# Attention maxima, depthwise taps and a scaling step: four edits in a fused block-and-attention kernel

## The chip, the cores and the metric

The kernel runs on one core of one Trainium2 chip. The time is the device time of one execution in microseconds (us). Engines are named as in the profile: TensorE is PE (its weight loads PEld), VectorE is DVE, ScalarE is ACT, GpSimd is POOL, and SyncE (SP) issues the transfers.

## What is computed

All data are float32. The input is `x` of shape (4, 64, 64, 256). Layer 0 is a block with a scan over windows of 2 x 2 pixels, a 3 x 3 depthwise convolution and a feed-forward part; layer 1 is full self-attention over the 4096 pixels of each image. Cut to what matters here (384 is the inner width):

```python
# layer 0
xz = layernorm(x) @ in_proj_W                 # 256 -> 2 x 384
x_proj, z = xz[..., :384], xz[..., 384:]
y_ssm  = 0.5 * (scan_fwd + scan_bwd)          # each: states over 4 pixels of a window, 8 states, plus x_proj * D
y_dw   = depthwise_3x3(x_proj)                # 9 taps per channel
y_conv = gelu(y_dw @ pw_W)
alpha  = sigmoid(gate)
y      = (alpha * y_ssm + (1 - alpha) * y_conv) * silu(z)
x_out  = x + y @ out_W
x1     = x_out + gelu(layernorm(x_out) @ fuse_W1 + b1) @ fuse_W2 + b2
# layer 1, per image, n = 4096
f, g, h = x1 @ Wf + bf, x1 @ Wg + bg, x1 @ Wh + bh      # 32, 32 and 256 wide
attn = softmax(g @ f.T, axis=-1)
out  = gamma * ((attn @ h) @ Wo + bo) + x1
```

## The kernel before

**Chunks.** Layer 0 works on 32 chunks of 8 rows (512 pixels, `TOK`), eight per image. In most of it channels lie on partitions, in `KI` = 3 blocks of 128. A chunk goes through `head` (layer norm, input projection to `xc`), `prepare` (the scan's parameters), `scan` (24 steps for each direction), `merge` (the scan's result `y` is transposed back and added into `xc`), and, one chunk behind, `conv` and `tail`. `halo` copies `xc` into the padded tile `xp`, which the depthwise taps read.

**Depthwise.** `depthwise` treats the three channel blocks in turn. A block with `f < dense` is computed on TensorE: each tap is a matmul with a diagonal weight, accumulated in one PSUM bank, which ScalarE copies out (L571). The other blocks run on VectorE, nine operations per block (L580, L582), each adding one tap. In the first image two blocks are dense, afterwards one. Blocks and taps are told apart by the tiles of the profile's rows: `q<-xp,dw` is the first dense block, `q<-xp,wide` the second.

**Tail.** Pointwise matmul (L613), GELU (L618), a scaling by `1 - alpha` on ScalarE (L625), then on VectorE a combined multiply and add with `alpha / 2` times the scan's result (L628), the gate (L631), the output projection (L638, added at L642), the feed-forward part (L658, L669, L673) and the projections that attention reads (`fgd`, `vod` in DRAM, L682 to L699).

**Attention in tiles beside the layer.** As soon as the first image is through layer 0, attention starts and layer 0 of the next images runs beside it. A tile is 128 queries. `weights` makes a tile's 4096 x 128 scores (L832) in two groups of four banks, copies them to SBUF (L840), folds the maxima over keys (L846, L848, last fold L851), transposes them (L854), reduces (L856), broadcasts (L858), spreads them over partitions by a matmul with the identity (L860), copies that out as `nb` (L862), and then adds it and takes the exponential in four pieces (L866, L867). `attend` multiplies the finished weights with the values (L1027, 32 matmuls a tile) in eight steps.

**Order.** The order of issue is written out by Python generators: each `yield` gives the cost, in us, of what was just issued. In each of its eight steps `attend` issues four value matmuls, takes one piece of the next tile's `weights` (`next(beside, None)`), and lets `fill(RATE)` issue layer-0 work worth 7.2 by those costs. `weights` has eight pieces, so it is done when `attend` is. A scheduler then settles each engine's order from this issue order. PSUM banks `q0` to `q3` are handed out in turn by `aside()`; `four()` takes all four.

**Late pairs.** When layer 0 has ended (checked at even tiles), the remaining queries go in pairs of tiles, 256 queries at a time: `late_weights` (scores L924, copies L932, maxima L937 and L944, transposes L947, broadcast L954, spread L958, copy L961, bias and exponential L964, L965) and `attend_late` (L1005).

Every value block is loaded from DRAM for every tile (`vt<-vod`), by SyncE, four blocks ahead.

Of the kernel before, what the change touches and what calls it, by code (L numbers as in the profile page):

```python
# [22 lines left out]
AF = mybir.ActivationFunctionType  # L23
ALU = mybir.AluOpType
# [4 lines left out]
P = 128  # L29
# [5 lines left out]
KI = INNER // P  # L35
# [3 lines left out]
ROWS = 8  # L39
# [20 lines left out]
def block_then_attention_kernel(  # L60
# [97 lines left out]
    def aside(shape=(P, TOK)):  # L158

        i = turn[0]  # L160
        turn[0] = (i + 1) % 4
        return pss.tile(list(shape), F32, tag=f"q{i}", name=f"q{i}")
# [384 lines left out]
    def merge(at):  # L547

        y = merged.pop(at)
        xc = heads[at][1]  # L550
        for f in range(KI):
            py = bank()
            for t in range(4):
                nc.tensor.transpose(py[:, t * P : (t + 1) * P], y[:, t, f * P : (f + 1) * P], ident)
            nc.vector.scalar_tensor_tensor(xc[:, f, :], xc[:, f, :], dsum[:, f : f + 1], py, ALU.mult, ALU.add)
            yield 1.1

    def depthwise(ydw, dense):

        for f in range(KI):  # L560
            if f < dense:
                pc = aside()
                for tap in range(9):
                    dy, dx = divmod(tap, 3)
                    nc.tensor.matmul(  # L565
                        pc, lhsT=diags[9 * f + tap], rhs=xp[:, f, dy : dy + ROWS, dx : dx + W],
                        start=(tap == 0), stop=(tap == 8),
                    )
                    if tap in (2, 5):
                        yield 2.6  # L570
                nc.scalar.copy(ydw[:, f, :], pc)  # L571
                yield 2.6
                continue
            o = ydw[:, f, :].rearrange("p (r c) -> p r c", r=ROWS)
            for tap in range(9):
                dy, dx = divmod(tap, 3)
                x_tap = xp[:, f, dy : dy + ROWS, dx : dx + W]
                w_tap = v("dw", 9 * f + tap)
                if tap == 0:
                    nc.vector.tensor_scalar(o, x_tap, w_tap, None, ALU.mult)  # L580
                else:
                    nc.vector.scalar_tensor_tensor(o, x_tap, w_tap, o, ALU.mult, ALU.add)  # L582
                if tap % 3 == 2:
                    yield 2.0
# [3 lines left out]
    def conv(at):  # L588
        b = at // NBLK
        ydw = one.tile([P, KI, TOK], F32, tag="ff", name="ydw")  # L590
        ydws[at] = ydw
        yield from depthwise(ydw, KI - 1 if b == 0 else 1)

    def next_head(at):

# [6 lines left out]
    def tail(at):  # L602
# [7 lines left out]
        for f in range(KI):  # L610
# [10 lines left out]
                    AF.Gelu,  # L621
                )
            yield 2.58
        for f in range(KI):
            nc.scalar.activation(yz[:, f, :], yz[:, f, :], AF.Copy, scale=one_a[:, f : f + 1])  # L625

        for f in range(KI):
            nc.vector.scalar_tensor_tensor(  # L628
                yz[:, f, :], s[:, f, :], half_a[:, f : f + 1], yz[:, f, :], ALU.mult, ALU.add
            )  # L630
            nc.vector.tensor_tensor(yz[:, f, :], yz[:, f, :], zs[:, f, :], ALU.mult)  # L631
            yield 1.3
# [177 lines left out]
    def load_values(b, q, n):  # L810

        vt = vp.tile([P, 2, DIM + 1], F32, tag="vt", name="vt")
        a = 2 * (n % 2) * (DIM + 1)
        nc.sync.dma_start(
            out=vt.rearrange("p t c -> p (t c)"), in_=vod[b * NBLK + n // 2][:, a : a + 2 * (DIM + 1)]
        )
        vts[b, q, n] = vt

    def weights(b, q, es):


        fQ, gq = quarters[b], gqs.pop((b, q))
        mx = one.tile([P, TOK], F32, tag="mx", name="mx")
        for g in range(2):
            pr = four()

            with tc.high_priority():
                last = None
                for s in range(4):
                    at = g * TOK + s * P  # L830
                    for r in range(4):
                        ins = nc.tensor.matmul(  # L832
                            pr[r][:, s * P : (s + 1) * P], lhsT=fQ[CK * r : CK * (r + 1), at : at + P],
                            rhs=gq[CK * r : CK * (r + 1), :], start=True, stop=True,
                        )
                        last = behind(ins, last)
            for a in range(2):
                e = ep.tile([P, 2, TOK], F32, tag="eq", name="eq")
                for j in range(2):
                    nc.scalar.copy(e[:, j, :], pr[2 * a + j])  # L840
                es.append(e)
            yield
            for r in range(4):
                e = es[2 * g + r // 2]
                if g == 0 and r == 0:
                    nc.vector.tensor_tensor(mx, e[:, 0, :], e[:, 1, :], ALU.max)  # L846
                elif g == 1 or r > 1:
                    nc.vector.tensor_tensor(mx, mx, e[:, r % 2, :], ALU.max)  # L848
            if g == 0:
                yield  # L850
        nc.vector.tensor_tensor(mx[:, :QB], mx[:, :QB], mx[:, QB:], ALU.max)  # L851
        pm = aside()
        for c in range(2):
            nc.tensor.transpose(pm[:, c * P : (c + 1) * P], mx[:, c * P : (c + 1) * P], ident)  # L854
        nm = st.tile([P, 1], F32, tag="nm", name="nm")
        nc.vector.tensor_reduce(nm, pm[:, :QB], AX.X, ALU.max, negate=True)  # L856
        nmb = two.tile([P, P], F32, tag="nb", name="nmb")
        nc.vector.tensor_copy(nmb, nm.to_broadcast([P, P]))  # L858
        pn = aside()
        nc.tensor.matmul(pn[:, :P], lhsT=nmb, rhs=ident, start=True, stop=True)  # L860
        nb = two.tile([P, P], F32, tag="nb", name="nb")
        nc.scalar.copy(nb, pn[:, :P])  # L862
        yield
        for n, e in enumerate(es):
            e8 = e.rearrange("p r (s q) -> p (r s) q", s=4)
            nc.vector.tensor_tensor(e8, e8, nb.unsqueeze(1).broadcast_to([P, 8, P]), ALU.add)  # L866
            nc.scalar.activation(e, e, AF.Exp)  # L867
            yield
# [32 lines left out]
    def load_late_values(b, q, n):  # L901

        g, r = divmod(n, 4)
        vt = vp.tile([P, 2, DIM + 1], F32, tag="vt", name="vt")
        a = 2 * (g % 2) * (DIM + 1)
        nc.sync.dma_start(
            out=vt.rearrange("p t c -> p (t c)"),
            in_=vod[b * NBLK + 4 * (g // 2) + r][:, a : a + 2 * (DIM + 1)],
        )
        vts[b, q, n] = vt  # L910

    def late_weights(b, q, odd, es):
# [42 lines left out]
        yield  # L955
        pn = aside()
        for c in range(2):
            nc.tensor.matmul(  # L958
                pn[:, c * P : (c + 1) * P], lhsT=wide[:, c, :], rhs=ident, start=True, stop=True
            )  # L960
        nc.scalar.copy(nb, pn[:, :QB])  # L961
        for n, e in enumerate(es):
            e4 = e.rearrange("p r s q -> p (r s) q")
# [46 lines left out]
                next(beside, None)  # L1010
        outcome(b, 2 * q, res, sums)

    def attend(b, q, es, beside, following):

        res = load_rest(b, q, two, "res", 1)
        acc = pso.tile([P, TOK], F32, tag="pso", name="acc")
        for k in range(NI):
            for h in range(2):
                n = 2 * k + h
                if n + 4 < 2 * NI:  # L1020
                    load_values(b, q, n + 4)
                else:
                    following(n + 4 - 2 * NI)
                vt = vts.pop((b, q, n))
                for s in range(2):
                    a = (2 * h + s) * P
                    nc.tensor.matmul(  # L1027
                        acc[:, : DIM + 1], lhsT=es[k // 2][:, k % 2, a : a + P], rhs=vt[:, s, :],
                        start=(n == 0 and s == 0), stop=(n == 2 * NI - 1 and s == 1),
                    )  # L1030
            next(beside, None)
            fill(RATE)
        outcome(b, q, res, [acc])
# [17 lines left out]
    for n in range(4):  # L1051
        load_values(0, 0, n)
    es = []
    for _ in weights(0, 0, es):
        fill(RATE)
    a = 0
    while True:
        b, q = divmod(a, NQ)
        b1, q1 = divmod(a + 1, NQ)
        if q1 == 0:  # L1060
            until((b1 + 1) * NBLK - 1)
        ahead = []
        late = ready["tail"] == LAST - 1 and q1 % 2 == 0
        if late:
            n0 = (b1, q1 // 2)
            load_late_queries(*n0)
            beside = twice(late_weights(*n0, 0, ahead))
            attend(b, q, es, beside, lambda n: load_late_values(*n0, n))
            es = ahead
            break  # L1070
        if q1 == 0:
            quarter(b1, one, "fQ")
        load_queries(b1, q1)
        attend(b, q, es, weights(b1, q1, ahead), lambda n: load_values(b1, q1, n))
        es = ahead
        a += 1
    odd, block = 0, n0
    while block:
# [98 lines left out]
```

## Time and profile before

| | |
|---|---|
| three runs | 5365.54 us median (5365.16 to 5367.03) |
| the profiled execution's own time | 5371.37 us |
| its span, first to last instruction | 5369.6 us |
| busy: PE, DVE, ACT | 5029.3, 4558.3, 3599.4 us |
| mean granted TensorE clock | 0.978 |
| chunk 0 to the start of attention | about 0 to 940 us |
| attention beside layer 0 | about 940 to 4430 us |
| last two tiles without layer work | about 4430 to 4492 us |
| late pairs | about 4492 to 5369.6 us |

A row of the profile's groups reads: line, engine, operation, output<-inputs, shapes, count, then busy us and mean ns of one, then the idle time of the engine just before such an instruction and what ended it. A float32 matmul shows as two instructions, a transpose as one. TensorE's busy time is modelled at the ends of matmuls, so a group's busy time (overlaps counted once) is the better measure of what it takes than its mean duration. A line of the waits reads: engine, tile and line that waited, `<-` what ended the wait, then us in total, times, longest.

### The profile page before, as it was taken

What the parts mean: (1) busy time and instruction counts of PE and PEld (TensorE: products, weight loads), DVE (VectorE), ACT (ScalarE), POOL (GpSimd) and SP (SyncE); (2) the same over time, 40 slices, a digit from 0 to 9 for tenths busy, and PEclk for the clock granted to TensorE, in tenths of its full rate; (3) what the DMA queues carried; (4) which work ended last, traced back from release to release, by engine and by line L of the source; (5) the groups of instructions that cost most, each with busy time, mean ns of one, the idle gap of its engine ahead of it and who ended that gap; (6) DMA issues with size and microseconds to landing.
All of it is one profiled execution on the core that took longest, in us unless ns stands there. A gap on an engine that the chain in (4) does not pass through costs nothing. (4 is left out here: it accounts for less than half of the span.)

```text
span 5369.6 us, 77772 instructions
## 1 busy us (share of the span) xinstructions
PE 5029.3 (94%) x27476; PEld 3585.9 (67%) x27476; DVE 4558.3 (85%) x8386; ACT 3599.4 (67%) x5530; POOL 206.0 (4%) x304
## 2 busy tenths in 40 slices
PE   7999999999999999999999999999999999999999
PEld 4555555666666666666666666666666667888887
DVE  7999999889988899889889998888998875666665
ACT  5767767778777677767777766767777744555554
POOL 0000000000000000000000000000000000000000
PEclk8999999999999999999999999999999999999999
DMA  1001001333333333333333333333343335555554
GB/s 47 26 30 31 19 25 31 98 109 107 115 113 112 114 112 114 118 115 107 111 116 111 115 116 107 114 114 113 102 123 113 110 116 165 146 146 146 146 146 138
DMA packets 333126, 558.45 MB, mean 104 GB/s; under 512 B 51904, under 2 KB 86976, under 8 KB 332736
## 3 DMA queue, kind: packets, MB, share of 16 engines
q1 hardware_dynamic: 330160, 551.52, 35.1%
q8 instruction: 217, 3.56, 0.3%
q10 hardware_dynamic: 2576, 1.97, 0.1%
q14 instruction: 173, 1.42, 0.1%
HBM read 494.49 MB, written 58.79 MB: 103 GB/s over the span
## 5 line engine op out<-in xcount | busy, mean ns | idle before, releaser
L1027 PE MATMUL acc<-vt,eq 128*128 128x257 f32 x4864 | 1234.2, 389 | 16.9 <-DVE res L975 13.0
L392 ACT ACTIVATE e<-dt,a_sc 128x384 f32<-128x384 f32 x1536 | 852.7, 611 | 347.0 <-PE bank L449 318.9
L1027 PEld LDWEIGHTS acc<-vt,eq 128*128 128x128 f32 x4864 | 891.1, 193 | 249.2 <-issue 116.6
L467 DVE SCALAR_TENSOR_TENSOR y<-p,bc,y 128x384 f32<-128x384 f32 x1536 | 948.8, 618 | 0.7
L449 PEld LDWEIGHTS bank<-ident,e 128*128 128x128 f32 x4320 | 524.3, 143 | 302.1 <-issue 125.7
L449 PE MATMUL bank<-ident,e 128*128 128x128 f32 x4320 | 647.8, 280 | 72.2 <-DVE p L461 29.3
L1005 PE MATMUL bank<-vt,eT 128*128 128x257 f32 x2496 | 625.8, 382 | 0.0
L476 DVE SCALAR_TENSOR_TENSOR h<-u,bc,p 128x384 f32<-128x384 f32 x1024 | 618.2, 621 | 0.1
L461 DVE TENSOR_TENSOR p<-bank,h 128x384 f32<-128x384 f32 x960 | 517.0, 552 | 52.4 <-PE bank L449 50.4
L1005 PEld LDWEIGHTS bank<-vt,eT 128*128 128x128 f32 x2496 | 467.1, 190 | 81.0 <-issue 12.9
L840 ACT COPY eq<-q 128x512 f32<-128x512 f32 x608 | 310.8, 593 | 179.7 <-PE q L832 166.4
L866 DVE TENSOR_TENSOR eq<-eq,nb 128x1024 f32<-128x1024 f32 x304 | 367.7, 1231 | 19.2 <-ACT nb L862 18.9
L867 ACT ACTIVATE eq<-eq 128x1024 f32<-128x1024 f32 x304 | 317.5, 1054 | 92.7 <-DVE eq L866 88.7
L937 DVE TENSOR_TENSOR mx<-mx,eT 128x512 f32<-128x512 f32 x364 | 252.0, 692 | 143.0 <-ACT eT L932 113.2
L848 DVE TENSOR_TENSOR mx<-mx,eq 128x512 f32<-128x512 f32 x456 | 317.0, 695 | 50.5 <-ACT eq L840 38.5
L932 ACT COPY eT<-q 128x512 f32<-128x512 f32 x416 | 213.2, 597 | 188.5 <-PE q L924 188.5
L392 ACT ACT_TABLE_LOAD x254 | 325.9, 1283 | 11.0 <-PE bank L449 6.8
L457 DVE SCALAR_TENSOR_TENSOR p<-bank,bc,u 128x384 f32<-128x384 f32 x480 | 294.1, 613 | 45.8 <-PE bank L449 45.6
L582 DVE SCALAR_TENSOR_TENSOR ydw<-xp,vec,ydw 128x512 f32<-128x512 f32 x448 | 325.4, 750 | 2.2
L613 PE MATMUL q<-ydw,wpw 128*128 128x512 f32 x576 | 269.3, 599 | 18.8 <-ACT eq L840 18.8
L964 DVE TENSOR_TENSOR eT<-eT,m 128x1024 f32<-128x1024 f32 x208 | 238.5, 1221 | 46.6 <-ACT m L961 46.6
L565 PE MATMUL q<-xp,dw 128*128 128x512 f32 x576 | 274.0, 597 | 2.4 <-ACT eq L840 2.4
(151 smaller groups left out, 7394.7 us busy)
## 6 DMA issues: line engine op xcount, KB each, us to landing
vt<-vod SPq DMA_DIRECT2D x1632, 257.0 KB, 2.8
vod<-vst SPq DMA_DIRECT2D x32, 514.0 KB, 4.4
xo<-in_x_dram SPq DMA_DIRECT2D x256, 64.0 KB, 2.7
xt<-in_x_dram SPq DMA_DIRECT2D x256, 64.0 KB, 1.9
x1d<-xo SPq DMA_DIRECT2D x32, 512.0 KB, 2.9
res<-x1d SPq DMA_DIRECT2D x76, 128.0 KB, 2.6
out_dram<-res SPq DMA_DIRECT2D x304, 32.0 KB, 1.6
fgd<-fg SPq DMA_DIRECT2D x32, 256.0 KB, 2.0
```

The costliest lines, as they stand in the source:

```text
L392: nc.scalar.activation(e[:, f, :], dts[d][:, f, lo : lo + 3 * P], AF.Exp, scale=a_sc[:, d, f * NST + n : f * NST + n + 1],)
L449: nc.tensor.transpose(pa[:, f * P : (f + 1) * P], es[d, n][:, f, off : off + P], ident)
L461: nc.vector.tensor_tensor(p, pa[:, :INNER], hs[d], ALU.mult)
L467: nc.vector.scalar_tensor_tensor(y[:, t, :], p, bc[:, t, d, NST + n : NST + n + 1], y[:, t, :], ALU.mult, ALU.add)
L476: nc.vector.scalar_tensor_tensor(hs[d], u[d][:, t, :], bc[:, t, d, n : n + 1], p, ALU.mult, ALU.add)
L582: nc.vector.scalar_tensor_tensor(o, x_tap, w_tap, o, ALU.mult, ALU.add)
L840: nc.scalar.copy(e[:, j, :], pr[2 * a + j])
L848: nc.vector.tensor_tensor(mx, mx, e[:, r % 2, :], ALU.max)
L866: nc.vector.tensor_tensor(e8, e8, nb.unsqueeze(1).broadcast_to([P, 8, P]), ALU.add)
L867: nc.scalar.activation(e, e, AF.Exp)
L1005: nc.tensor.matmul(sums[c][:, : DIM + 1], lhsT=e[:, r % 2, s, c * P : (c + 1) * P], rhs=vt[:, s, :], start=(n == 0 and s == 0), stop=(n == ...
L1027: nc.tensor.matmul(acc[:, : DIM + 1], lhsT=es[k // 2][:, k % 2, a : a + P], rhs=vt[:, s, :], start=(n == 0 and s == 0), stop=(n == 2 * NI ...
```

## The change

There are four edits.

1. `weights` gets a `yield` between the last fold of the maxima and their transposes. It then has nine pieces for eight steps. `attend` therefore receives the tile's own generator as `own` and takes its last piece in its first step, ahead of the next tile's first piece. The first tile's generator is still run to its end before the first `attend`, with one more `fill`.
2. The spread of the maxima over partitions is a TensorE transpose instead of a matmul with the identity as the moving operand, in `weights` and in `late_weights`.
3. In the second to fourth images the dense block does taps 0 to 6 on TensorE; taps 7 and 8 are done on VectorE, the first of them reading the bank. The copy L571 is left out there. The costs yielded change from three times 2.6 to 2.6, 2.6 and 2.0 per block. In the first image all nine taps stay on TensorE, with the copy issued after the third yield instead of before it.
4. `merge` ends with ScalarE scaling `xc` by `alpha / 2`; the scaling by `1 - alpha` in `tail` is left out, and VectorE's combined operation multiplies the GELU's result by `1 - alpha` and adds the scaled `xc`.

```diff
--- before.py
+++ after.py
@@ -554,30 +554,36 @@
                 nc.tensor.transpose(py[:, t * P : (t + 1) * P], y[:, t, f * P : (f + 1) * P], ident)
             nc.vector.scalar_tensor_tensor(xc[:, f, :], xc[:, f, :], dsum[:, f : f + 1], py, ALU.mult, ALU.add)
             yield 1.1
-
-    def depthwise(ydw, dense):
+        for f in range(KI):
+            nc.scalar.activation(xc[:, f, :], xc[:, f, :], AF.Copy, scale=half_a[:, f : f + 1])
+
+    def depthwise(ydw, dense, taps):
 
         for f in range(KI):
             if f < dense:
                 pc = aside()
-                for tap in range(9):
+                for tap in range(taps):
                     dy, dx = divmod(tap, 3)
                     nc.tensor.matmul(
                         pc, lhsT=diags[9 * f + tap], rhs=xp[:, f, dy : dy + ROWS, dx : dx + W],
-                        start=(tap == 0), stop=(tap == 8),
+                        start=(tap == 0), stop=(tap == taps - 1),
                     )
-                    if tap in (2, 5):
+                    if tap % 3 == 2:
                         yield 2.6
-                nc.scalar.copy(ydw[:, f, :], pc)
-                yield 2.6
-                continue
+                if taps == 9:
+                    nc.scalar.copy(ydw[:, f, :], pc)
+                    continue
             o = ydw[:, f, :].rearrange("p (r c) -> p r c", r=ROWS)
-            for tap in range(9):
+            for tap in range(taps if f < dense else 0, 9):
                 dy, dx = divmod(tap, 3)
                 x_tap = xp[:, f, dy : dy + ROWS, dx : dx + W]
                 w_tap = v("dw", 9 * f + tap)
                 if tap == 0:
                     nc.vector.tensor_scalar(o, x_tap, w_tap, None, ALU.mult)
+                elif f < dense and tap == taps:
+                    nc.vector.scalar_tensor_tensor(
+                        o, x_tap, w_tap, pc.rearrange("p (r c) -> p r c", r=ROWS), ALU.mult, ALU.add
+                    )
                 else:
                     nc.vector.scalar_tensor_tensor(o, x_tap, w_tap, o, ALU.mult, ALU.add)
                 if tap % 3 == 2:
@@ -589,7 +595,7 @@
         b = at // NBLK
         ydw = one.tile([P, KI, TOK], F32, tag="ff", name="ydw")
         ydws[at] = ydw
-        yield from depthwise(ydw, KI - 1 if b == 0 else 1)
+        yield from depthwise(ydw, KI - 1 if b == 0 else 1, 9 if b == 0 else 7)
 
     def next_head(at):
 
@@ -621,12 +627,10 @@
                     AF.Gelu,
                 )
             yield 2.58
-        for f in range(KI):
-            nc.scalar.activation(yz[:, f, :], yz[:, f, :], AF.Copy, scale=one_a[:, f : f + 1])
 
         for f in range(KI):
             nc.vector.scalar_tensor_tensor(
-                yz[:, f, :], s[:, f, :], half_a[:, f : f + 1], yz[:, f, :], ALU.mult, ALU.add
+                yz[:, f, :], yz[:, f, :], one_a[:, f : f + 1], s[:, f, :], ALU.mult, ALU.add
             )
             nc.vector.tensor_tensor(yz[:, f, :], yz[:, f, :], zs[:, f, :], ALU.mult)
             yield 1.3
@@ -849,6 +853,7 @@
             if g == 0:
                 yield
         nc.vector.tensor_tensor(mx[:, :QB], mx[:, :QB], mx[:, QB:], ALU.max)
+        yield
         pm = aside()
         for c in range(2):
             nc.tensor.transpose(pm[:, c * P : (c + 1) * P], mx[:, c * P : (c + 1) * P], ident)
@@ -857,7 +862,7 @@
         nmb = two.tile([P, P], F32, tag="nb", name="nmb")
         nc.vector.tensor_copy(nmb, nm.to_broadcast([P, P]))
         pn = aside()
-        nc.tensor.matmul(pn[:, :P], lhsT=nmb, rhs=ident, start=True, stop=True)
+        nc.tensor.transpose(pn[:, :P], nmb, ident)
         nb = two.tile([P, P], F32, tag="nb", name="nb")
         nc.scalar.copy(nb, pn[:, :P])
         yield
@@ -955,9 +960,7 @@
         yield
         pn = aside()
         for c in range(2):
-            nc.tensor.matmul(
-                pn[:, c * P : (c + 1) * P], lhsT=wide[:, c, :], rhs=ident, start=True, stop=True
-            )
+            nc.tensor.transpose(pn[:, c * P : (c + 1) * P], wide[:, c, :], ident)
         nc.scalar.copy(nb, pn[:, :QB])
         for n, e in enumerate(es):
             e4 = e.rearrange("p r s q -> p (r s) q")
@@ -1010,7 +1013,7 @@
                 next(beside, None)
         outcome(b, 2 * q, res, sums)
 
-    def attend(b, q, es, beside, following):
+    def attend(b, q, es, own, beside, following):
 
         res = load_rest(b, q, two, "res", 1)
         acc = pso.tile([P, TOK], F32, tag="pso", name="acc")
@@ -1028,6 +1031,7 @@
                         acc[:, : DIM + 1], lhsT=es[k // 2][:, k % 2, a : a + P], rhs=vt[:, s, :],
                         start=(n == 0 and s == 0), stop=(n == 2 * NI - 1 and s == 1),
                     )
+            next(own, None)
             next(beside, None)
             fill(RATE)
         outcome(b, q, res, [acc])
@@ -1051,7 +1055,8 @@
     for n in range(4):
         load_values(0, 0, n)
     es = []
-    for _ in weights(0, 0, es):
+    own = weights(0, 0, es)
+    for _ in own:
         fill(RATE)
     a = 0
     while True:
@@ -1065,14 +1070,15 @@
             n0 = (b1, q1 // 2)
             load_late_queries(*n0)
             beside = twice(late_weights(*n0, 0, ahead))
-            attend(b, q, es, beside, lambda n: load_late_values(*n0, n))
+            attend(b, q, es, own, beside, lambda n: load_late_values(*n0, n))
             es = ahead
             break
         if q1 == 0:
             quarter(b1, one, "fQ")
         load_queries(b1, q1)
-        attend(b, q, es, weights(b1, q1, ahead), lambda n: load_values(b1, q1, n))
-        es = ahead
+        beside = weights(b1, q1, ahead)
+        attend(b, q, es, own, beside, lambda n: load_values(b1, q1, n))
+        es, own = ahead, beside
         a += 1
     odd, block = 0, n0
     while block:
```

## The prediction

> **What bounds the kernel now.** I read the busy line of the page first, then the busy time by stage, then the waits inside the long middle stage, then the rows of the operations that the change touches.
>
> ```profile
> PE 5029.3 (94%) x27476; PEld 3585.9 (67%) x27476; DVE 4558.3 (85%) x8386; ACT 3599.4 (67%) x5530; POOL 206.0 (4%) x304
> ```
>
> TensorE (PE) is the busiest, VectorE (DVE) next. The stages differ, so the second view cuts the span at 940 us (attention starts beside the first layer), at 4430 us (the layer has ended) and at 4492 us (the late pairs start). The columns are length, then PE, weight loads, DVE, ACT and POOL busy, then granted clock and DMA share.
>
> ```profile
> 0.00:940.00 940.00, 845.98 (x3588) 525.06 (x3589) 868.24 (x1766) 666.51 (x1075) 55.78 (x87) 0.94 0.10 30
> 940.00:4430.00 3490.00, 3254.34 (x18459) 2304.22 (x18457) 3103.46 (x5784) 2476.72 (x3783) 150.22 (x217) 0.98 0.38 112
> 4430.00:4492.00 62.00, 58.36 (x353) 43.50 (x352) 33.74 (x50) 25.64 (x41) 0.00 (x0) 0.92 0.67 201
> 4492.00:5369.60 877.60, 870.65 (x5080) 713.11 (x5078) 552.87 (x788) 430.52 (x633) 0.00 (x0) 1.00 0.50 144
> ```
>
> The first stage is VectorE's (92% busy, PE 90%). The last is TensorE's alone (99%, DVE 63%). In the middle stage TensorE is at 93% and VectorE at 89%: TensorE leads, but relief of TensorE that is paid for on VectorE cannot count in full. TensorE's 236 us of idle time there, and ScalarE's (ACT) waits for TensorE, are read from the waits of that window (who waited for whom: us, times, longest).
>
> ```profile
> PE q L854 <- DVE mx L851: 37.3, 30, 3.2
> PE q L613 <- ACT eq L840: 18.8, 15, 2.3
> PE bank L449 <- DVE p L457: 16.7, 11, 2.4
> PE bank L449 <- DVE p L461: 15.6, 12, 2.9
> ...
> ACT nb L862 <- PE q L860: 88.5, 44, 5.7
> ...
> ACT ydw L571 <- PE q L565: 43.6, 20, 7.6
> ```
>
> TensorE's largest single wait is for the fold of the maxima (L851), in front of the transposes (L854). Two other lines matter: ScalarE stands 88.5 us before the copy that ends the spread of the maxima, and 43.6 us before the copy that ends a TensorE depthwise chunk. VectorE mostly runs behind TensorE: the output projection's add (L642) follows 12 matmuls of 128x256, yet waits for them only 9 times in 48.
>
> The rows of the operations concerned (count, then busy us and mean ns of one):
>
> ```profile
> L582 DVE SCALAR_TENSOR_TENSOR ydw<-xp,vec,ydw 128x512 f32<-128x512 f32 x448 | 325.4, 750 | 2.2
> L565 PE MATMUL q<-xp,dw 128*128 128x512 f32 x576 | 274.0, 597 | 2.4 <-ACT eq L840 2.4
> L625 ACT ACTIVATE yz<-yz,one_a 128x512 f32<-128x512 f32 x96 | 65.2, 716 | 0.4
> L860 PE MATMUL q<-ident,nmb 128*128 128x128 f32 x152 | 33.1, 300 | 6.0 <-DVE nmb L858 5.5
> L854 PE MATMUL q<-ident,mx 128*128 128x128 f32 x152 | 31.1, 287 | 37.7 <-DVE mx L851 37.5
> L571 ACT COPY ydw<-q 128x512 f32<-128x512 f32 x40 | 23.4, 584 | 63.8 <-PE q L565 63.8
> ```
>
> **What the Trainium skill says.** "Perfetto Trace Analysis", section "Transposes", asks that logical transposes use transpose and not a standard matmul, since a transpose skips arithmetic. The trace agrees: 76 spreads by matmul (L860) are 152 instructions and 33.1 us, or 0.436 us each; 152 transposes of the same shape (L854) are 152 instructions and 31.1 us, or 0.205 us each. "VectorE: DVE Perf Modes", section "The perf-mode tier table", puts fp32 two-tensor operations at 1x wherever the operand lies. The trace agrees that PSUM costs nothing extra: the merge's operation reads a bank and takes 747 ns (L555), the tap from SBUF takes 750. "TensorE: Matmul & The Clock Gate", section "Architectural detail: the array is 16× 32×32, not 1× 128×128", says that VectorE and ScalarE keep strict queue order; the two waits of ScalarE above show what that costs whatever stands behind.
>
> **The change part by part.** All sums are changes of the profiled run, 5371.4 us (span 5369.6). The median of the runs is 5365.5, 0.11% lower; I apply the changes to the median.
>
> *Two taps.* In chunks 8 to 31 (24 of 32), 2 of 9 dense taps leave TensorE. A tap is two instructions of the L565 row: 274.0 us over 288 taps is 0.951 us. 24 x 2 x 0.951 = **-45.7 us** of TensorE, all in the middle stage. VectorE gets 48 operations at 0.750: +36.0 us, 1.0% of that stage. ScalarE loses 24 copies at 0.584: -14.0 us, and the 43.6 us wait with them. VectorE's slack is 387 us there, but its queue is in order, so part of the 36 reaches TensorE as later data: bounds 0 and 36, I take half, **+18**. The first new operation reads the bank directly behind the last dense matmul. VectorE then waits where ScalarE did: bounds 0 and 24 x 43.6/20 = 52 us. I take 0, for VectorE runs behind and only one matmul, not three, is issued between the last step's end and the read. Behind it in VectorE's queue stand the scan's operations, for which TensorE's transposes (L449) and ScalarE's exponentials wait; the bank it holds is next wanted by the scores (L832).
>
> *Spread by transposes.* 76 spreads fall from 0.436 to 0.205: about 74 x 0.231 = -17.1. In the late pairs (L958) 52 spread matmuls of 15.9 us (0.306 each) become the kind of L947 (10.0 us for 52, 0.192): 54 x 0.114 = -6.1, on the engine that sets that stage. **-23.2 us**. Nothing is added.
>
> *The step.* The fold is issued one step earlier than transposes, reduction, broadcast, spread and copy. A tile takes 8 steps (47.3 us, so 5.9 a step), and VectorE has that long to finish the fold: the 37.3 us can go. What is late next is the spread, which waits for reduction and broadcast (0.42 + 0.22 us) on the same lagging queue; before, TensorE had already waited that lag out at L854. Bounds: 0 and -37.3 us; I take half, **-19**. The ninth step carries one bias add (1.23 us) and one exponential (1.05 us) into the next tile's first step. They are first read at its seventh, some 35 us later: 0, bounded by +2.3 us a tile if that cover failed. The step issues no DMA, passes none on SP and nothing on POOL; the value loads keep their places.
>
> *Scaling moved.* 96 activations of 0.716 us leave the tail and 96 enter the merge, so ScalarE's sum stands. VectorE's 9.8 us wait for L625 may go, with 13.8 us of unattributed waits at the same line. In the merge ScalarE waits for VectorE, with copies of the next chunk's inputs (L409) behind it: at most one 0.75 us operation a chunk, +24 us. Bounds -24 and +24; I take 0. The built program also has 6 fewer table loads of 1.28 us on ScalarE: 0.
>
> *Fewer tiles beside the layer.* The new steps count less cost (7.2 instead of 7.8 per dense chunk), and the first tile's ninth step draws layer work forward. In the built program the accumulations fall from 2432 to 2368, two tiles fewer, and the late pairs rise from 26 to 27. The two tiles stood after the layer's end: in TensorE's terms 2 x (1234.2 + 194.0 + 64.2)/76 = 39.3 us, against 877.6/26 = 33.8 for a pair: **-5.5 us** (bounds -10 and +5).
>
> *The copy after its yield* in chunks 0 to 7 only lets other ScalarE work pass it (its wait there was 20.2 us) in a stage that VectorE sets: 0, bounds -10 and +10.
>
> Sum: -45.7 + 18 - 23.2 - 19 - 5.5 = **-75.4 us**. From 5371.4 that is 5296; from the median, **5290 us**.
>
> **The rivals.**
> - *VectorE's part is hidden and the fold's wait goes whole*: -45.7 - 23.2 - 37.3 - 5.5 = -111.7, so 5254 us. For it: VectorE's slack of 387 us. Against it: TensorE already waits for VectorE's scan results.
> - *The waits only move*: the spread takes over the fold's wait and VectorE's 36 us come through in full: -45.7 - 23.2 - 5.5 + 36 = -38.4, so 5327 us. For it: the reduction is queued on the same engine that made the fold late.
> - *VectorE stalls at the new tap, and the kernel gets slower.* In the middle stage the bank read takes over ScalarE's wait (52 us) and adds its 36 us: 88 us more on VectorE. Against 74.4 us taken from TensorE, with no fold gain, that is +13.9: 5379 us. It decides once over 84% of the 88 reaches TensorE. For it: the taps' read stands right behind its producer. Against it: L642.
> - That nothing of it happens is excluded: the built program has 240 in place of 288 such dense matmuls, and fold and transposes stand apart.
>
> **How the numbers follow.** A measurement of this kernel can tell 0.2%, about 11 us, from no change. Main case 0.43; all gains 0.13; waits moved 0.22; between that and the stall, within 0.2%, 0.08; the stall 0.14. So faster 0.78, same 0.08, slower 0.14. The range runs from 5240 (all gains, with some of the scaling's and the copy's bounds) to 5360, which leaves out the stall, most of the no-change case and little below.
>
> **What would show it.** In the profile after: dense L565-type matmuls down to 480 instructions at about 0.48 us each; VectorE's middle-stage share up from 89 to about 91%; the wait for the fold below 5 us, and the wait before the spread's transpose below 20; the new bank read waiting for TensorE under 15 us in all; TensorE's share of the middle stage not below 92%. The prediction is wrong if that bank read waits 40 us or more with TensorE's share falling, if the spread's transpose idles for 35 us or more, or if the late stage takes more than 34 us a pair.

## The result, and the profile after

The changed kernel takes 5293.27 us (median of 4 runs, 5291.23 to 5299.24), the kernel before 5366.28 on the same chip. The ratio is 0.9866, with a 95% interval of 0.9849 to 0.9883: 73 us less, against the 75.4 us of the prediction's sum. The total came out; several of the terms behind it did not, and the experiments below are mostly about that.

The busy line of the page after:

```profile
PE 4958.2 (94%) x27186; PEld 3545.8 (67%) x27186; DVE 4574.8 (86%) x8433; ACT 3573.8 (68%) x5499; POOL 205.4 (4%) x304
```

TensorE is busy 71 us less and VectorE 16 us more. Next is the busy time by stage, cut at events and not at fixed times: the first scores, which end the part that image 1 has to itself (912 us in the kernel before, not the 940 of the earlier cut), layer 0's last values stored, and the first value matmuls of the late pairs. Between the last two lie the lone tiles, which run after layer 0 has ended. Columns are length, then PE, weight loads, DVE, ACT and POOL busy, granted clock, DMA share and rate.

```profile
0.00:889.00 889.00, 811.41 (x3451) 502.14 (x3455) 836.24 (x1715) 643.03 (x1039) 54.60 (x87) 0.96 0.10 31
889.00:4362.00 3473.00, 3223.82 (x18370) 2291.86 (x18363) 3149.35 (x5877) 2474.34 (x3785) 150.79 (x217) 0.98 0.38 112
4362.00:4388.00 26.00, 25.07 (x152) 18.69 (x151) 15.14 (x26) 9.69 (x19) 0.00 (x0) 1.00 0.75 225
4388.00:5292.20 904.20, 897.90 (x5224) 733.07 (x5223) 574.09 (x818) 446.71 (x657) 0.00 (x0) 1.00 0.50 145
```

The kernel before, cut at the same events, for the first two stages:

```profile
0.00:912.00 912.00, 822.84 (x3443) 511.53 (x3443) 840.44 (x1714) 644.42 (x1039) 55.78 (x87) 0.94 0.10 30
912.00:4429.00 3517.00, 3276.48 (x18603) 2317.14 (x18604) 3130.56 (x5835) 2498.80 (x3818) 150.22 (x217) 0.98 0.38 112
```

With the events read to a tenth, one profiled execution each (us):

| stage | before | after | change | by the prediction's terms |
|---|---|---|---|---|
| image 1 | 911.9 | 888.6 | -23.3 | 0 |
| attention beside layer 0 | 3517.4 | 3473.9 | -43.5 | -63.8 |
| lone tiles + late pairs | 63.6 + 876.7 | 25.8 + 903.9 | -10.6 | -11.6 |
| sum | 5369.6 | 5292.2 | -77.4 | -75.4 |

The last column takes -45.7 + 18 - 17.1 - 19 for the middle, and -5.5 - 6.1 for the end. A third of the gain sits in a stage for which I had predicted none, and the middle stage gave 20 us less than I had said.

The rows of the operations concerned, after:

```profile
L588 DVE SCALAR_TENSOR_TENSOR ydw<-xp,vec,ydw 128x512 f32<-128x512 f32 x472 | 338.4, 743 | 1.2
L567 PE MATMUL q<-xp,dw 128*128 128x512 f32 x480 | 230.4, 594 | 2.3 <-ACT eq L844 2.3
...
L859 PE MATMUL q<-ident,mx 128*128 128x128 f32 x148 | 29.0, 278 | 9.0 <-DVE mx L855 8.9
L865 PE MATMUL q<-ident,nmb 128*128 128x128 f32 x74 | 22.5, 304 | 12.7 <-DVE nmb L863 12.4
L584 DVE SCALAR_TENSOR_TENSOR ydw<-xp,vec,q 128x512 f32<-128x512 f32 x24 | 17.7, 739 | 0.0
L963 PE MATMUL q<-ident,nmb 128*128 128x128 f32 x54 | 10.4, 274 | 0.0
```

The dense matmuls are 480 at 0.480 us each (230.4/480). The new tap that reads the bank (L584) waits for nothing. The wait for the fold, the last figure of L859, is 8.9 us instead of 37.5. The spread (L865) is 74 instructions for 74 tiles, 0.304 us each. TensorE's longest waits in the middle stage are now these (us, times, longest):

```profile
PE bank L449 <- DVE p L457: 26.8, 23, 3.1
PE bank L449 <- DVE p L461: 20.1, 14, 4.8
PE q L368 <- DVE bc L353: 19.7, 11, 2.8
...
PE q L865 <- DVE nmb L863: 12.4, 12, 2.5
```

The first two are the scan's transposes, waiting for VectorE's scan products. They stood at 17.8 and 15.6 us before, in the stage cut at 912 us.

### The profile page after: what moved, and what is told of

Same layout as the page of the kernel before. It is cut to its first block, busy times and chain, and to the rows that moved or that the text cites. A ratio compares the mean times of both kernels' runs of the same rounds, so it can differ in the third digit from the quotient of the medians.

```text
span 5292.2 us, 77188 instructions
## 1 busy us (share of the span) xinstructions
PE 4958.2 (94%) x27186; PEld 3545.8 (67%) x27186; DVE 4574.8 (86%) x8433; ACT 3573.8 (68%) x5499; POOL 205.4 (4%) x304
## 5 line engine op out<-in xcount | busy, mean ns | idle before, releaser
L1030 PE MATMUL acc<-vt,eq 128*128 128x257 f32 x4736 | 1207.0, 391 | 25.3 <-DVE res L978 12.3
L392 ACT ACTIVATE e<-dt,a_sc 128x384 f32<-128x384 f32 x1536 | 851.9, 611 | 357.0 <-PE bank L449 350.3
L1030 PEld LDWEIGHTS acc<-vt,eq 128*128 128x128 f32 x4736 | 874.0, 194 | 256.2 <-issue 121.1
L467 DVE SCALAR_TENSOR_TENSOR y<-p,bc,y 128x384 f32<-128x384 f32 x1536 | 938.0, 611 | 0.4
L449 PEld LDWEIGHTS bank<-ident,e 128*128 128x128 f32 x4320 | 522.5, 143 | 323.9 <-issue 123.5
L449 PE MATMUL bank<-ident,e 128*128 128x128 f32 x4320 | 648.8, 280 | 81.1 <-DVE p L461 38.6
L1008 PE MATMUL bank<-vt,eT 128*128 128x257 f32 x2560 | 645.8, 382 | 0.0
L1008 PEld LDWEIGHTS bank<-vt,eT 128*128 128x128 f32 x2560 | 478.6, 189 | 83.7 <-issue 13.9
L937 ACT COPY eT<-q 128x512 f32<-128x512 f32 x432 | 221.4, 597 | 198.7 <-PE q L929 198.7
L588 DVE SCALAR_TENSOR_TENSOR ydw<-xp,vec,ydw 128x512 f32<-128x512 f32 x472 | 338.4, 743 | 1.2
L457 DVE SCALAR_TENSOR_TENSOR p<-bank,bc,u 128x384 f32<-128x384 f32 x480 | 291.6, 607 | 23.3 <-PE bank L449 23.0
L1008 PE MATMUL acc<-vt,eT 128*128 128x257 f32 x896 | 273.9, 388 | 0.0
```

The source lines that it names most:

```text
L392: nc.scalar.activation(e[:, f, :], dts[d][:, f, lo : lo + 3 * P], AF.Exp, scale=a_sc[:, d, f * NST + n : f * NST + n + 1],)
L449: nc.tensor.transpose(pa[:, f * P : (f + 1) * P], es[d, n][:, f, off : off + P], ident)
L467: nc.vector.scalar_tensor_tensor(y[:, t, :], p, bc[:, t, d, NST + n : NST + n + 1], y[:, t, :], ALU.mult, ALU.add)
L1008: nc.tensor.matmul(sums[c][:, : DIM + 1], lhsT=e[:, r % 2, s, c * P : (c + 1) * P], rhs=vt[:, s, :], start=(n == 0 and s == 0), stop=(n == ...
L1030: nc.tensor.matmul(acc[:, : DIM + 1], lhsT=es[k // 2][:, k % 2, a : a + P], rhs=vt[:, s, :], start=(n == 0 and s == 0), stop=(n == 2 * NI ...
```

## The experiments

Four edits, two questions: which of them carries the 73 us, and do they add up? First each edit is made alone on the kernel before. Then the taps, the step and the scaling are each taken away from the kernel after, and a third tap is moved; the spread was never taken away. Last come two of the pairs and the order of issue. By the prediction's sum, each edit brings its own price wherever it stands. A rival is that the issue order itself, which each edit shifts, moves the time: a `yield` with another cost changes what lies beside what. The three groups ran on three chips. Ratios and differences, in the table and in the text, are against the kernel before on the same chip (5368.36, 5370.14 and 5366.69 us).

| kernel | us | ratio (95%) | difference, us |
|---|---|---|---|
| step alone | 5361.56 | 0.9987 (0.9981 to 0.9994) | -7 |
| spread alone | 5364.39 | 0.9992 (0.9984 to 1.0001) | -4 |
| taps alone | 5381.76 | 1.0029 (1.0017 to 1.0040) | +13 |
| scaling alone | 5331.31 | 0.9933 (0.9920 to 0.9945) | -37 |
| after, nine taps on TensorE | 5296.06 | 0.9863 (0.9849 to 0.9876) | -74 |
| after, without the step | 5328.79 | 0.9923 (0.9911 to 0.9936) | -41 |
| after, scaling back in the tail | 5332.09 | 0.9929 (0.9917 to 0.9942) | -38 |
| after, three taps on VectorE | 5299.27 | 0.9865 (0.9850 to 0.9880) | -71 |
| step and spread | 5346.50 | 0.9962 (0.9950 to 0.9975) | -20 |
| step and scaling | 5320.99 | 0.9914 (0.9900 to 0.9927) | -46 |
| taps alone, dense costs kept | 5370.94 | 1.0005 (0.9997 to 1.0013) | +4 |
| dense cost changed, no work moved | 5381.39 | 1.0026 (1.0016 to 1.0035) | +15 |

Stage lengths and waits below come from one profiled execution of each kernel. Some of these lie above their median: the kernel before by 6 us, the scaling alone by 7, the taps alone by 10. A few us between two stages may therefore be noise.

### The scaling alone

```diff
 # merge, at its end
+        for f in range(KI):
+            nc.scalar.activation(xc[:, f, :], xc[:, f, :], AF.Copy, scale=half_a[:, f : f + 1])
 # tail
-        for f in range(KI):
-            nc.scalar.activation(yz[:, f, :], yz[:, f, :], AF.Copy, scale=one_a[:, f : f + 1])
-                yz[:, f, :], s[:, f, :], half_a[:, f : f + 1], yz[:, f, :], ALU.mult, ALU.add
+                yz[:, f, :], yz[:, f, :], one_a[:, f : f + 1], s[:, f, :], ALU.mult, ALU.add
```

> The kernel before with the scaling moved from the tail into the merge alone; tiles 76. Theory A (the prediction's): 0 us, within 24 either way. Theory E (it is what made image 1 shorter in the profile after, by taking three activations out of the chain from GELU to output projection): -20 us or more, attention starting near 890 us, and VectorE's wait for the output projection in the first stage (12 us) gone.

It gave -37 us, the largest single effect, from the edit that I had costed at nothing. Theory E came true. Of the 33 us by which the two profiled spans differ, 23.7 lie in image 1 (911.9 to 888.2), which the after kernel shortens by the same amount. The timeline of the kernel before shows one chunk's tail there (start us, us, engine, line, what, count, then in brackets the idle time before and what ended it):

```profile
259.77 1.28 ACT L392 ACT_TABLE_LOAD   x1
...
261.06 1.12 ACT L392 ACTIVATE e<-dt,a_sc 128x384 f32<-128x384 f32 x2
...
262.09 1.93 ACT L625 ACTIVATE yz<-yz,one_a 128x512 f32<-128x512 f32 x3
...
262.83 1.41 DVE L628 SCALAR_TENSOR_TENSOR yz<-xc,half_a,yz 128x512 f32<-128x512 f32 x2 [0.35 <-ACT yz L625]
263.93 1.61 ACT L392 ACTIVATE e<-dt,a_sc 128x384 f32<-128x384 f32 x3
...
264.58 0.48 PE L449 MATMUL pa<-ident,e 128*128 128x128 f32 x1 [1.66 <-ACT e L392]
...
270.56 0.69 DVE L642 TENSOR_TENSOR xo<-q,xo 128x512 f32<-128x512 f32 x1 [1.27 <-PE q L638]
```

The same place with the scaling moved:

```profile
257.61 1.43 DVE L628 SCALAR_TENSOR_TENSOR yz<-yz,one_a,xc 128x512 f32<-128x512 f32 x2
...
258.94 1.28 ACT L392 ACT_TABLE_LOAD   x1
...
260.23 2.64 ACT L392 ACTIVATE e<-dt,a_sc 128x384 f32<-128x384 f32 x5
...
265.65 0.69 DVE L642 TENSOR_TENSOR xo<-q,xo 128x512 f32<-128x512 f32 x1
```

Before, the three scalings (1.93 us) stand in ScalarE's queue between the second and the third exponential of the next scan (L392). Two chains are late by it. VectorE's combined operation waits for a scaling (0.35 us) and with it the output projection, so the add at L642 comes 10.8 us after the table load begins. TensorE's transpose (L449) idles 1.66 us for the third exponential. With the scaling moved, the exponentials run through, L628 starts before the table load, and L642 comes 6.7 us after the load begins, without a wait. That is 4.1 us sooner in this chunk; the stage gains 23.7 us over eight chunks, 3.0 each. VectorE's waits in image 1 had this line in the kernel before; in this one it is gone.

```profile
DVE xo L642 <- PE q L638: 12.0, 8, 2.3
```

The chunk is typical. In all eight chunks of image 1 the three scalings stand among these exponentials, behind the second in six chunks and behind the third in the first and the last. Table loads, which could have been a rival cause, are 138 on ScalarE in image 1 with and without the move.

The granted clock moves too. Here are 12 us of the kernel before and the same stretch here, each in halves:

```profile
256.00:262.00 6.00, 3.05 (x22) 2.15 (x20) 6.00 (x13) 5.93 (x8) 0.00 (x0) 0.90 0.01 1
262.00:268.00 6.00, 4.34 (x13) 3.03 (x13) 5.65 (x10) 6.00 (x12) 0.00 (x0) 0.53 0.00 0
```

```profile
254.00:260.00 6.00, 4.20 (x22) 2.75 (x22) 6.00 (x12) 5.91 (x9) 0.00 (x0) 0.93 0.01 1
260.00:266.00 6.00, 6.00 (x25) 4.72 (x24) 5.96 (x12) 5.33 (x11) 0.00 (x0) 0.79 0.00 0
```

Before, TensorE is busy for 3.05 of 6 us and then has a clock of 0.53. Over image 1 the clock is 0.94 before and 0.96 here, or 112.6 and 71.7 us at half clock. How much of the 23.7 us is the queue and how much the clock, no run separates. TensorE's busy time in image 1 sets a limit: for the same instructions it fell from 822.8 to 810.1 us, so a faster TensorE can account for about 13 us at most, as far as the modelled ends of matmuls can be trusted. The rest is idle time that went. In the merge, where the scaling arrives, ScalarE waits for VectorE in front of it for 3.8 us in the whole kernel; I had feared 24.

### The scaling put back

```diff
-        for f in range(KI):
-            nc.scalar.activation(xc[:, f, :], xc[:, f, :], AF.Copy, scale=half_a[:, f : f + 1])
 # and the tail as before
```

> The changed kernel with the scaling back in the tail; tiles 74. Additive theory and theory I-a: 37 us slower than the changed kernel, near 5330 us, of which 23 in image 1 (attention starting near 912 us). Theory I-b (the taps need the scaling's move): 65 to 75 us slower, near 5365 us.

Put back into the kernel after, the scaling leaves -38 of -73 us, so it costs 35: image 1 is 912.7 us again, 24.1 more than after, and the middle 13.3 more. Made alone and taken away last, the edit is worth the same. It is the one edit that adds up.

### The taps alone, and the taps taken away

```diff
 # alone: depthwise(ydw, dense, taps) as in the change; the rest as before
-        yield from depthwise(ydw, KI - 1 if b == 0 else 1)
+        yield from depthwise(ydw, KI - 1 if b == 0 else 1, 9 if b == 0 else 7)
 # taken away from the kernel after
-        yield from depthwise(ydw, KI - 1 if b == 0 else 1, 9 if b == 0 else 7)
+        yield from depthwise(ydw, KI - 1 if b == 0 else 1, 9)
```

> The kernel before with the depthwise edit alone (taps 7 and 8 of images 2 to 4 on VectorE, the copy after its yield in image 1); tiles 74. Theory A (the prediction's): -45.7 from TensorE, +18 from VectorE, -5.5 from the exchange of tiles: about -33 us, start of attention unchanged at 912 us. Theory B (VectorE's stall at the bank read): slower by 14 us or more, with the bank read waiting over 40 us. Theory D (the copy after its yield shortens image 1): a further -20 us, and attention starts near 890 us.

> The changed kernel with all nine taps of the dense block on TensorE again (step, spread and scaling kept; the bank is copied out by ScalarE); tiles 74. Additive theory (single effects measured alone: step -7, spread -4, taps +13, scaling -37): it should be 13 us faster than the changed kernel. Theory I (the taps pay only together with another edit): 25 us slower than the changed kernel or more, near 5320 us.

Alone the taps cost 13 us. In the kernel after they are worth nothing: it stands at -73 with them and at -74 without, and the ratios (0.9866 and 0.9863) lie within each other's intervals. So neither theory for the second kernel came true, not the 13 us gained and not the 25 lost. In the taps alone image 1 is 911.7 us against 911.9, so issuing the copy after its yield does nothing there, as predicted. The middle stage of the kernel after with nine taps:

```profile
889.00:4369.00 3480.00, 3258.58 (x18490) 2309.97 (x18491) 3122.23 (x5833) 2475.64 (x3800) 149.83 (x217) 0.98 0.38 113
```

Against the kernel after, TensorE has 34.8 us more to do here (3258.6 to 3223.8), of the 45.7 in my sum, but 27.8 us less idle time (221.4 against 249.2). The stage is 7 us longer, the whole profiled execution 1.5. Most of TensorE's relief has turned into waits.

### One tap more

```diff
-        yield from depthwise(ydw, KI - 1 if b == 0 else 1, 9 if b == 0 else 7)
+        yield from depthwise(ydw, KI - 1 if b == 0 else 1, 9 if b == 0 else 6)
```

> The changed kernel with three taps of the dense block on VectorE instead of two; tiles 74. Theory A (TensorE still sets the middle stage): 22.8 us less on TensorE, half of 18 us more coming through from VectorE: 10 to 15 us faster, about 5280 us. Theory F (VectorE, at 91% there, now sets the pace as much as TensorE): no change within 10 us, or slower, with VectorE's share above 92% and TensorE's below 92%.

Three taps on VectorE are no better than two or none: with nine, seven and six taps on TensorE the ratios are 0.9863, 0.9866 and 0.9865. That is theory F's time, but not its signs: VectorE's share of the middle stage is 90.9% and TensorE's 92.5%, where it had said above and below 92%.

### Is it the work or the order of issue?

The taps alone cost 13 us, though nothing waits at the new tap. The edit also changes the costs that the dense block yields, so it shifts the order. Two kernels separate these: the taps' work with the old cost, and the new cost without any work moved.

```diff
 # taps alone, dense costs kept
-                    yield 2.0
+                    yield 2.6 if f < dense else 2.0
 # kernel before, cost changed only
                 nc.scalar.copy(ydw[:, f, :], pc)
-                yield 2.6
+                yield 2.6 if dense == 2 else 2.0
```

> The depthwise edit alone as in only_taps, but with the block's last yield at 2.6 instead of 2.0, so that the costs that place layer work between attention steps stay as they were; tiles 76. Theory O (what made the taps alone slower is the order of issue that the changed cost led to, not the work on VectorE): within 10 us of the kernel before. Theory V (VectorE's extra work, and TensorE's waits for it): slower by 13 us or more again.

> The kernel before with only the dense block's last yield at 2.0 instead of 2.6 in images 2 to 4: no instruction of a chunk changes, only where layer work falls between the attention steps, and two lone tiles become a late pair; tiles 74. If order matters little: -10 us, from the exchange of tiles alone. Theory O (order by itself moves the middle stage by tens of us): another 10 us or more, in either direction.

The work alone is +4 us, not to be told from nothing; the cost alone, without any operation of a chunk changed, is +15. So theory O holds: the loss of the taps alone lies with the order that the new cost leads to. The middle stages of the two:

```profile
915.00:4432.00 3517.00, 3245.82 (x18502) 2301.80 (x18498) 3154.99 (x5881) 2483.89 (x3794) 149.45 (x217) 0.98 0.37 112
```

```profile
915.00:4448.00 3533.00, 3284.68 (x18568) 2324.03 (x18569) 3127.64 (x5832) 2525.91 (x3836) 150.56 (x217) 0.98 0.37 111
```

The first has 31 us less TensorE work than the kernel before (3276.5) in a stage of the same length, 3517 us. One place where it went is the wait for the fold in that kernel, 37.3 us in the kernel before:

```profile
PE q L858 <- DVE mx L855: 50.7, 32, 3.4
```

The second has as much VectorE work as the kernel before in 16 us more time. It runs 74 tiles beside the layer instead of 76, and this exchange for a late pair saved it 10.1 us (63.6 + 876.7 to 20.4 + 909.8). That small term I had at -5.5; the step alone shows -10.6 and the taps alone -7.9.

### The step alone, and taken away

```diff
 # weights
         nc.vector.tensor_tensor(mx[:, :QB], mx[:, :QB], mx[:, QB:], ALU.max)
+        yield
 # attend, in each step
+            next(own, None)
             next(beside, None)
```

> The kernel before with the extra step alone (a yield between fold and transposes, with the tile's last piece carried into its own first step). Theory A (the prediction's step): TensorE's 37 us wait for the fold goes, about half of it returns in front of the spread: -19 us, and the exchange of two lone tiles for a late pair gives another -5.5, so about -25 us, all of it after 940 us. Theory B (the wait only moves): TensorE idles in front of the spread for 35 us or more, and only the exchange is left: -5 us. In both, the start of attention stays at about 912 us.

> The changed kernel without the extra step; tiles 74. Additive theory: 7 us slower than the changed kernel. Theory I-a (the taps need the step, because a later VectorE makes the fold later, and without the step TensorE waits for it): about 35 to 45 us slower, near 5335 us, with TensorE's wait for the fold back at 40 us or more. Theory I-b (they need the scaling's move instead): about 7 us slower.

Alone it is worth 7 us, no more than its exchange of tiles (10.6 us); its middle stage is 3514.1 us against 3517.4. That is the time of theory B, but not its sign, for the spread's wait stays far below 35 us. The wait for the fold has shrunk, as the lines show:

```profile
PE q L861 <- DVE nmb L859: 15.5, 14, 3.0
...
PE q L855 <- DVE mx L851: 8.3, 3, 3.0
```

The 29 us taken from that wait went into others: the spread's (5.5 to 15.5), the gate's matmuls (L328, 9.3 to 19.5) and those of the scan's parameters (L368, 12.9 to 19.3), among others. TensorE's idle time in the stage is 238.8 us against 240.5. Taken away from the kernel after, the same edit costs 32 us: the middle stage is 38 us longer (3511.7 against 3473.9), and the fold's wait is back:

```profile
PE q L858 <- DVE mx L855: 42.5, 31, 3.1
```

This is near the time and the wait of theory I-a. Its reason, that the taps need the step, cannot be the whole of it: with all nine taps of the dense block on TensorE, step, spread and scaling together make -74 as well, against -48 for the sum of their single effects. Taken away from the kernel after, step and scaling cost 32 and 35 us, together most of the 73.

### The spread alone, and the pairs

```diff
-        nc.tensor.matmul(pn[:, :P], lhsT=nmb, rhs=ident, start=True, stop=True)
+        nc.tensor.transpose(pn[:, :P], nmb, ident)
 # and the same in late_weights
```

> The kernel before with the spread of the maxima by transposes alone, in tiles and late pairs; tiles stay 76. Theory A (the prediction's): 0.231 us less per tile spread and 0.114 per late one: -23 us. Theory C (from the profile after, where an isolated spread transpose took 0.304 us of TensorE): -10 us beside the layer and -6 in the late pairs, -16 us.

> The kernel before with the extra step and the spread by transposes, no other edit; tiles 74. Additive theory: -7 - 4 = -11 us, near 5358 us. Theory S (step and spread pay only together, since with the step the spread is what TensorE waits at): about -38 us, near 5331 us.

> The kernel before with the extra step and the scaling's move, no other edit; tiles 74. Additive theory and theory S: -7 - 37 = -44 us, near 5324 us. Theory T (step and scaling pay together): about -70 us, near 5298 us.

Alone the spread gives -4 us, within the interval of nothing. Its rows:

```profile
L860 PE MATMUL q<-ident,nmb 128*128 128x128 f32 x76 | 23.1, 304 | 6.3 <-DVE nmb L858 5.7
...
L958 PE MATMUL q<-ident,nmb 128*128 128x128 f32 x52 | 10.0, 274 | 0.0
```

L860 fell from 33.1 to 23.1 us and L958 from 15.9 to 10.0. The late stage shortened with its row, 876.7 to 869.4 us; the middle stage, 3518.9 us, did not. With the step in place it is worth more: step and spread give -20, 13 beyond the step. On top of step and scaling, the kernel with nine taps (-74) stands 28 us beyond -46; besides the spread it has only the copy after its yield. That showed nothing in image 1, but in images 2 to 4, where this kernel has it too, it was not tested by itself.

The four edits alone add up to -7 - 4 + 13 - 37 = -35 us; together they make -73. Among step, spread and scaling the pairs give -20 (sum of singles -11) and -46 (sum -44), all three -74 (sum -48). So part of the surplus (9 us) comes with step and spread, and most of it only when all three are there; the pair of spread and scaling was not run, so it is not shown that all three are needed. The cause of the surplus stays open: every edit but the spread also shifts the order of issue, which alone made 15 us, and no run holds the order fixed while the edits change.

## Why the prediction was right, and where only its sum was

The forecast, faster with 5290 us, came within 3.3 us. That closeness is luck: errors of opposite sign cancelled. The term that I had priced highest, the taps, brought nothing, and the edit that I had priced at 0 brought about half of the gain.

- *Scaling moved*, taken as 0: it gave -37 alone and 35 when undone, beyond its own bound of 24. ScalarE's sum did stand; the failing step is to set the gain and the loss of bounded waits against each other and "I take 0". I looked for what waits behind the scaling where it arrives, in the merge, and not for what stood behind it where it left: the exponentials of the next scan in ScalarE's queue.
- *Two taps*, predicted -27.7: worth nothing in the kernel after, and +4 alone with the costs kept. TensorE's saving is real in its busy time (31 and 35 us of 45.7). The failing step is "I take half" of VectorE's 36 us: most of the saving went into waits, with VectorE at 89 to 91% of the stage (that its load is the reason is argued, not shown). My bound for that, all 36 us, which leaves -9.7, was closer than the half I took. That nothing waits at the bank read was right.
- *The step*, predicted -19, with -5.5 for the tiles: 7 us alone, 32 at the end. The fold's wait and its successor were named rightly (8.9 and 12.4 us; I had said below 5 and below 20), but a wait's length is not what its removal is worth: 29 us removed brought about 3 in the middle stage in one kernel, and in another the return of 34 us (8.9 to 42.5) cost 38.
- *Spread by transposes*, predicted -23.2: the late part, -6.1, measured -7.3. The other was priced with the wrong row: transposes in pairs take 0.205 us each, one alone 0.304. That makes 74 x (0.436 - 0.304) = -9.8 instead of -17.1, and alone even that did not shorten the middle stage (3518.9 us).
- *Fewer tiles*: -8 to -11 instead of -5.5, at its bound of -10, in the three kernels in which nothing else touches that part. In the changed kernel the end gave -10.6 for this and the late spread together.
- The rival *VectorE stalls at the new tap* is refuted by L584's wait of 0.0 and by three taps costing no more than two. *The waits only move* was close to the truth for the step alone and for the taps, though its total (5327 us) was not.

Of the signs, the dense row, VectorE's share (3149.35/3473 = 90.7%), the spread's wait, TensorE's share (92.8%) and the late stage (903.9/27 = 33.5 us a pair) came as said; the fold's wait missed by 3.9 us.

No kernel here is clearly better than the changed one; with nine taps left on TensorE it is equal, so that edit could be dropped.

## What to carry to other kernels

Where an operation leaves a queue that runs in order, ask what stood behind it there: 1.93 us of scaling ahead of another chain's exponentials cost 3 us per chunk, though ScalarE had the same work before and after. Work moved from an engine at 93% to one at 89% in the same stage came back as waits. Where the order of issue comes from costs, run a change of cost without work before crediting an edit with a few tenths of a per cent (here 0.26%), and take an edit away from the end version as well as trying it alone: the step was worth 7 us one way and 32 the other.

## What was not expected of the hardware

The granted clock fell after a stretch in which TensorE was still half busy: 3.05 of 6 us, the longest pause there 1.31 us, then 0.53 for 6 us. The Trainium skill ("TensorE: Matmul & The Clock Gate", section "What's actually happening") has the half clock come after at least one idle window of about 3.4 us; this trace shows it without an idle stretch of that length. In this example TensorE did only transposes after 256.05 us, so transposes might simply not count as work for the clock. The whole kernel before speaks against that as the only reason. It has 43 stretches at half clock. In the 3.4 us ahead of them TensorE's longest pause was under 3 us in 40 cases, and in 29 even if its transposes are counted as pauses. What nearly all share is a half-busy TensorE: at most 2.05 of those 3.4 us in 41 cases. The clock came back only after full work: TensorE was busy for at least 3.0 us of the last 3.4 of each stretch at half clock, but for the one in which the kernel ends.

Time at half clock in the middle stage was 112.6 us in the kernel before and 194.6 with the taps alone, in its slowest execution of six. How much of that kernel's +13 us comes this way was not isolated.
